# Four graph layers on one core: layer 1's first norm with centred weights, two-operation Sturm steps, and a wider window beside the last group of layer 0

## The chip, the cores and the metric

The kernel runs on one core of a Trainium2 chip. The metric is the device time of one execution in microseconds (us). The program is one launch; everything is fp32. The core has five engines that work side by side, each through its own queue in order: TensorE (PE, with the loads of its stationary operand shown apart as PEld), VectorE (DVE), ScalarE (ACT), GpSimd (POOL) and SyncE (SP), which here issues the DMAs.

## The reference, cut to what matters

128 graphs of 64 nodes with 256 features share one 64 x 64 weighted adjacency matrix. Four layers follow, each of the form x + f(relu(layernorm(x))).

```python
def _L0_gnn_ref(x, adj, ...):           # two graph convolutions, then LSTMs over windows of 1, 2, 3 and 4 nodes
    h = relu(einsum('ts,bsh->bth', adj, x @ Wg0 + bg0))
    h = relu(einsum('ts,bsh->bth', adj, h @ Wg1 + bg1))
    for p in range(1, MAX_SKIP + 1):
        ...                             # the last state of each window replaces that node's row of h
def _L1_gnn_ref(x, L, adjacency, Wc, bc, g1, be1, ...):
    lam_max = eigvalsh(L)[-1] + 1e-08
    L_norm = 2.0 * L / lam_max - eye(N)
    h = einsum('mn,bnf->bmf', L_norm, x) @ Wc + bc
    h = relu(_layernorm(h, g1, be1))
    x1 = h + x
    ...                                 # attention of 4 heads, layernorm, MLP with gelu, layernorm
def _L2_gnn_ref(h, adj_matrix, W, a):   # graph attention: softmax over neighbours
    ...
def _L3_gnn_ref(features, A, W1, b1, W2, b2):
    ...
    _, U = eigh(L_norm)                 # all 64 eigenvectors of the normalised Laplacian
    agg = einsum('mn,bnd->bmd', U.T, features)
    out = relu(agg @ W1 + b1) @ W2 + b2
    return einsum('nm,bmd->bnd', U, out)
```

## The kernel before, in words

**A planner writes the order.** The kernel first records all operations (`Plan.record`, from line 114) with their engine, group, tiles and dependencies. Then `Plan.schedule` (line 227) lays them out as a list scheduler, with a cost for each kind of operation (`Plan.cost`, line 176), and `issue` (line 338) emits them in that order. So each engine's queue is the planner's order, and every instruction carries line 344 in the profile: one tells groups apart by their tiles, not by lines. The planner picks for each engine the operation that can start first, and among those that can start at once the one of the lowest rank (line 328). An operation that depends on one of its own engine is planned to start at that one's end, some 0.11 us behind its cost.

**Groups.** Layer 0 works on 8 groups (0 to 7, NG = 8) of 8 tiles of 128 rows. The weights of layers 1 to 3 are prepared in one group of their own (WEIGHTS), layer 2's attention tiles are cleared in another (ATTN), and layers 1 to 3 run on 16 groups of 4 tiles (REST onward), each from its input to its output. The eigenvalue work (EIG) is a group aside, of the lowest rank on all engines but TensorE: it fills gaps of VectorE beside layer 0.

**The window.** `window(oldest)` (line 968) says how far ahead of the oldest unfinished group others may begin. While layer 0's last group (7), WEIGHTS or ATTN is the oldest, it gives `REST + 1 - oldest`: one group of layers 1 to 3 may work, and the loads of one more may be issued. After that it is 8 groups.

**Buffers.** The pool "big" has 12 tiles of 128 x 1024, and gets more as others are done with their memory: 10 in `arena` when the EIG group has ended, and those in whh[3], sums and mids (lines 963 to 966) when all of layer 0 has ended. While a layer-0 group is the oldest, 7 big tiles and 3 of the 8 PSUM banks are kept in reserve for it (`reserve`, line 971).

**Layer 0's memory for later weights.** Wc, Wq, Wk and Wv are loaded into the memory of Wih1, which the LSTM of windows of two (p = 1) has read for the last time; Wo and row vectors (bc, g1, be1, ...) into Wih2, further vectors and small tiles into Whh2, which windows of three (p = 2) read last. WEIGHTS needs the finished eigenvectors for `ursum` and `C3` (lines 1428 to 1434), so it ends after EIG.

**Sturm sweeps** (lines 634 to 663), in EIG: bisection finds the eigenvalues. Each of 9 sweeps evaluates, for 3 x 7 shifts on 64 partitions, a recurrence of 64 steps: a product DX x PL[k], from the second step on also a product PL[k-1] x E2 and a difference, each on 64 x 21 elements, and every eighth step a rescaling. Then the sign changes are counted.

**Layer 1's first norm** (lines 1523 to 1535). `relu_norm` makes h, `mix_fm` multiplies by the scaled Laplacian (`lapb`), `proj_tm` by Wc, two tiles of 256 columns into one PSUM bank, and VectorE adds bc on the way to x1. Then `norm(x1)`: `ln_stats` (line 1195) issues for each tile bn_stats and bn_aggr on VectorE, then four small operations on GpSimd (one of them the power -0.5), and ScalarE applies scale and bias to four tiles. VectorE multiplies by g1, GpSimd adds be1, VectorE takes the maximum with 0 and adds h.

Of the kernel before, what the change touches and what calls it, by code (L numbers as in the profile page):

```python
# [8 lines left out]
ALU = mybir.AluOpType  # L9
AF = mybir.ActivationFunctionType  # L10
AX = mybir.AxisListType

N = 64
KS = 7
# [332 lines left out]
def eig_decomp(plan, room, adj, adjT, ident, idf, ones):  # L347
# [17 lines left out]
    def scope():  # L365
        inner.reset([0])
        return inner
# [4 lines left out]
    def W(shape, name, bufs=None):  # L372

        if bufs is None:
            bufs = 2 if shape[-1] < N or name == "lab" else 1
        ring = kept.setdefault((name, tuple(shape)), [])
        if len(ring) < bufs:
            ring.append(room.tile(shape))
        else:
            ring.append(ring.pop(0))  # L380
        return ring[-1]
# [245 lines left out]
    V.tensor_copy(lo, l1.to_broadcast([N, 3]))  # L627
    C = 3 * KS
    ph = scope()
    PL = ph.tile([N, N + 1, C])  # L630
    V.memset(PL[:, 0, :], 1.0)
    DX = ph.tile([N, N, 3, KS])
    SG = ph.tile([N, N + 1, C])
    for s_ in range(NSWEEP):
        V.tensor_scalar(w, w, 1.0 / (KS + 1), None, op0=ALU.mult)
        x = W([N, 3, KS], 'x')
        V.tensor_scalar(x, c['ramp'], w, None, op0=ALU.mult)
        V.tensor_add(x, x, lo.unsqueeze(2).to_broadcast([N, 3, KS]))
        for l in range(3):
            V.tensor_mul(DX[:, :, l, :], BM[:, l, :].unsqueeze(2).to_broadcast([N, N, KS]), x[:, l, :].unsqueeze(1).to_broadcast([N, N, KS]))  # L640
            V.tensor_sub(DX[:, :, l, :], DM[:, l, :].unsqueeze(2).to_broadcast([N, N, KS]), DX[:, :, l, :])
        DXf = DX.rearrange('p k l s -> p k (l s)')
        for k in range(N):
            V.tensor_mul(PL[:, k + 1, :], DXf[:, k, :], PL[:, k, :])
            if k:
                b = W([N, 3, KS], 'b', 2)
                V.tensor_mul(b, PL[:, k - 1, :].rearrange('p (l s) -> p l s', l=3), E2[:, :, k - 1:k].to_broadcast([N, 3, KS]))
                V.tensor_sub(PL[:, k + 1, :], PL[:, k + 1, :], b.rearrange('p l s -> p (l s)'))
            if k % 8 == 7 and k < N - 1:
                mm = W([N, C], 'mm')  # L650
                V.tensor_reduce(mm, PL[:, k:k + 2, :].rearrange('p k c -> p c k'), op=ALU.max, axis=AX.X, apply_absolute_value=True)
                V.tensor_scalar(mm, mm, 1e-30, None, op0=ALU.max)
                V.reciprocal(mm, mm)
                V.tensor_mul(PL[:, k:k + 2, :], PL[:, k:k + 2, :], mm.unsqueeze(1).to_broadcast([N, 2, C]))
        V.tensor_scalar(SG, PL, 0.0, None, op0=ALU.is_lt)
        NE = DXf
        V.tensor_tensor(NE, SG[:, 1:, :], SG[:, :N, :], op=ALU.not_equal)
        ct = W([N, 3, KS], 'ct')
        V.tensor_reduce(ct.rearrange('p l s -> p (l s)'), NE.rearrange('p k c -> p c k'), op=ALU.add, axis=AX.X)
        V.tensor_tensor(ct, ct, li.unsqueeze(2).to_broadcast([N, 3, KS]), op=ALU.is_le)  # L660
        sm = W([N, 3], 'sm')
        V.reduce_sum(sm, ct, axis=AX.X)
        V.scalar_tensor_tensor(lo, sm, w, lo, op0=ALU.mult, op1=ALU.add)
# [269 lines left out]
def gnn_kernel(ctx: ExitStack, tc: tile.TileContext, a, out):  # L933
# [32 lines left out]
    more(mids, tuple(range(NG)))  # L966

    def window(oldest):
        return max(oldest, 0) + 2 - oldest if oldest < NG - 1 else REST + 1 - oldest if oldest < REST else 8

    def reserve(kind, oldest):
        if oldest < NG:
# [204 lines left out]
    def tm(n=HT, f=D):  # L1177

        return plan.value("big")[:, :n * f].rearrange("p (t f) -> p t f", f=f)
# [214 lines left out]
    ctile = lambda shape, src: load(room.tile(shape), src)  # L1394
    Wc, Wq, Wk, Wv, W1, W2, Wo = (wtile(a[n]) for n in ("Wc", "Wq", "Wk", "Wv", "W1", "W2", "Wo"))
    bc, g1, be1, bo, g2, be2, b2, g3, be3 = (btile(a[n]) for n in ("bc", "g1", "be1", "bo", "g2", "be2", "b2", "g3", "be3"))
    b1 = ctile([P, 4], a["b1"])

    g2c, be2c = (ctile([P, 2], a[n].rearrange("o (c p) -> p (o c)", p=P)) for n in ("g2", "be2"))
# [98 lines left out]
    def norm(t):  # L1498

        sc, bi = ln_stats(t)  # L1500
        for i in range(HT):
            ACT.activation(t[:, i, :], t[:, i, :], AF.Identity, scale=sc(i), bias=bi(i))
# [20 lines left out]
    def layer1(x):  # L1523
        h = relu_norm(x)
        lx = mix_fm(h, lambda t: lapb)
        x1 = tm()
        for t0 in (0, 2):
            ps = proj_tm(lambda c, t: lx[:, c, tok(t)], Wc, 2, t0)
            V.tensor_add(x1[:, t0:t0 + 2, :], ps.rearrange("p (t f) -> p t f", t=2), vec(bc, 2))
        norm(x1)  # L1530
        for t0 in (0, 2):
            xp, hp = x1[:, t0:t0 + 2, :], h[:, t0:t0 + 2, :]
            V.tensor_mul(xp, xp, vec(g1, 2))
            G.tensor_add(xp, xp, vec(be1, 2))
            V.scalar_tensor_tensor(xp, xp, 0.0, hp, op0=ALU.max, op1=ALU.add)
        x1T = to_fm(x1)
        qT, kT, v = fm(), fm(), tm()
        R = pieces(lambda c, n: x1T[:, c, n * HT * P // 2:(n + 1) * HT * P // 2], G)
        proj_fast(fastp["Wq"], R, qT)
        proj_fast(fastp["Wk"], R, kT)  # L1540
        for t0 in (0, 2):
            evac(pair(v, t0), proj_tm(lambda c, t: x1T[:, c, tok(t)], Wv, 2, t0), 1)
        for t0 in (0, 2):
            G.tensor_add(x1[:, t0:t0 + 2, :], x1[:, t0:t0 + 2, :], vec(bo, 2))


        ps = [bank("qk") for m in range(2)]
        with plan.burst():
            for b, m, r in [(b, m, r) for b in range(2 * HT) for m in range(2) for r in range(2)]:
                PE.matmul(ps[m][half(r ^ m), bat(b)], qT[half(r), m, bat(b)], kT[half(r), m, bat(b)], start=True, stop=True)  # L1550
        s = tm(4 * HT, N)
        for m in range(2):
            sm = s[:, m * 2 * HT:(m + 1) * 2 * HT, :]
            V.scalar_tensor_tensor(sm, ps[m].rearrange("p (b k) -> p b k", k=N), 0.125, vec(mask1, 2 * HT), op0=ALU.mult, op1=ALU.add)
            stat = plan.value("stat")
            softmax_shift(sm, stat[:, :2 * HT])
            ACT.activation(sm, sm, AF.Exp)
            ssum = stat[:, 2 * HT:4 * HT]
            V.reduce_sum(ssum, sm, axis=AX.X)
            V.reciprocal(ssum, ssum)  # L1560
            G.tensor_mul(sm, sm, ssum.unsqueeze(2).to_broadcast([P, 2 * HT, N]))

        pT = fm()
        for m in range(2):
            evac(pT[:, m, :], transposes([flat(s[:, (m * HT + t) * 2:(m * HT + t) * 2 + 2, :]) for t in range(HT)]), 1)
        oT = fm()

        po = [bank("o") for i in range(2)]
        with plan.burst():
            for m, t, i, r in [(m, t, i, r) for m in range(2) for t in range(HT) for i in range(2) for r in range(2)]:  # L1570
                PE.matmul(po[i][half(r), bat(m * HT + t)], v[half(i), t, bat(2 * m + r)], pT[half(i), m, bat(2 * t + (r ^ m))], start=True, stop=True)
        for i in range(2):
            evac(oT.rearrange("p c (t b n) -> p c t b n", t=HT, b=2)[:, :, :, i, :], po[i].rearrange("p (c t n) -> p c t n", c=2, t=HT), 1)
        x2 = tm()
        for t0 in (0, 2):
            ps = proj_tm(lambda c, t: oT[:, c, tok(t)], Wo, 2, t0)
            V.tensor_add(x2[:, t0:t0 + 2, :], ps.rearrange("p (t f) -> p t f", t=2), x1[:, t0:t0 + 2, :])
        norm(x2)
        x2T = fm()
        for c in range(2):  # L1580
            ACT.activation(x2T[:, c, :], transposes([x2[:, t, tok(c)] for t in range(HT)]), AF.Identity, scale=g2c[:, c:c + 1], bias=be2c[:, c:c + 1])
        V.tensor_mul(x2, x2, vec(g2))
        for t0 in (0, 2):
            G.tensor_add(x2[:, t0:t0 + 2, :], x2[:, t0:t0 + 2, :], vec(b2, 2))
        mT = [fm() for i in range(2)]
        for m in range(4):
            ACT.activation(mT[m // 2][:, m % 2, :], proj_fm(W1, x2T, m), AF.Gelu, bias=b1[:, m:m + 1])
        for t0 in (0, 2):
            ps = proj_tm(lambda c, t: mT[c // 2][:, c % 2, tok(t)], W2, 4, t0)
            V.tensor_add(pair(x2, t0), ps, pair(x2, t0))  # L1590
        for t0 in (0, 2):
            G.tensor_add(x[:, t0:t0 + 2, :], x[:, t0:t0 + 2, :], vec(be3, 2))
        norm(x2)
        for t0 in (0, 2):
            V.tensor_mul(x2[:, t0:t0 + 2, :], x2[:, t0:t0 + 2, :], vec(g3, 2))
            V.tensor_add(x[:, t0:t0 + 2, :], x[:, t0:t0 + 2, :], x2[:, t0:t0 + 2, :])
# [115 lines left out]
```

## Time and profile before

| | us |
|---|---|
| median of 3 runs | 2153.46 (2152.71 to 2155.54) |
| the profiled execution, its own time | 2151.09 |
| its span, from the first to the last instruction | 2149.3 |

| engine | busy us | instructions |
|---|---|---|
| PE (TensorE, matmuls) | 2102.0 | 16772 |
| PEld (loads of the stationary operand) | 1665.0 | 16772 |
| DVE (VectorE) | 1796.7 | 7434 |
| ACT (ScalarE) | 1124.1 | 2465 |
| POOL (GpSimd) | 708.4 | 1040 |

An fp32 matmul instruction leaves two records, so 16772 records are about twice the number of instructions. A row of a group of instructions gives the total busy time in which overlaps count once, the mean length of one in ns, and the idle time of the engine before them with what ended it. In the chain of waits, each piece is what the next one waited for. Layer 0's last matmuls end about 1361 us after the start of the span; layers 1 to 3 fill the rest.

### The profile page before, as it was taken

What the parts mean: (1) busy time and instruction counts of PE and PEld (TensorE: products, weight loads), DVE (VectorE), ACT (ScalarE), POOL (GpSimd) and SP (SyncE); (2) the same over time, 40 slices, a digit from 0 to 9 for tenths busy, and PEclk for the clock granted to TensorE, in tenths of its full rate; (3) what the DMA queues carried; (4) which work ended last, traced back from release to release, by engine and by line L of the source; (5) the groups of instructions that cost most, each with busy time, mean ns of one, the idle gap of its engine ahead of it and who ended that gap; (6) DMA issues with size and microseconds to landing.
All of it is one profiled execution on the core that took longest, in us unless ns stands there. A gap on an engine that the chain in (4) does not pass through costs nothing.

```text
span 2149.3 us, 46200 instructions
## 1 busy us (share of the span) xinstructions
PE 2102.0 (98%) x16772; PEld 1665.0 (77%) x16772; DVE 1796.7 (84%) x7434; ACT 1124.1 (52%) x2465; POOL 708.4 (33%) x1040
## 2 busy tenths in 40 slices
PE   9999999999999999999999999999999999999998
PEld 6688688688778778778778788877777877887776
DVE  5788888888999999989989898767787789876787
ACT  3354354355345345345345444566667666665783
POOL 7211211310110110110110002696556657864353
PEclk9999999999999999999999999999999999999999
DMA  5000100100100100100000111200000100000001
GB/s 206 1 3 22 42 2 22 41 1 21 40 1 21 40 1 21 40 1 21 26 1 21 50 40 51 90 1 2 21 22 21 41 22 21 11 12 11 2 2 60
DMA packets 44868, 57.70 MB, mean 27 GB/s; under 512 B 8928, under 2 KB 38496, under 8 KB 44640
## 3 DMA queue, kind: packets, MB, share of 16 engines
q1 hardware_dynamic: 43536, 53.71, 7.6%
q8 instruction: 131, 2.15, 0.4%
q10 hardware_dynamic: 1104, 1.05, 0.2%
q14 instruction: 97, 0.79, 0.1%
HBM read 37.53 MB, written 16.78 MB: 25 GB/s over the span
## 4 chain that ended last, share of the span: by engine, by line
PE 79%; DVE 11%; POOL 3%; issue 3%; ACT 2%; DMA 2%; SPq 0%; DVEq 0%; ACTq 0%; POOLq 0%
PE bank L344 79%; DVE stat L344 3%; DVE arena L344 3%; DVE big L344 3%; POOL stat L344 2%; DVE mids L344 1%; DVE sums L344 1%; DMA big<-in_x_dram 1%; ACT big L344 1%; ACT mids L344 1%; POOL arena L344 0%; ACT arena L344 0%; POOL big L344 0%; DVE Whh L344 0%; SPq L344 0%
## 5 line engine op out<-in xcount | busy, mean ns | idle before, releaser
L344 PE MATMUL bank<-big,Wih 128*128 128x256 f32 (+3 forms) x2408 | 731.7, 426 | 14.7 <-DVE arena L344 6.9
L344 PEld LDWEIGHTS bank<-big,Wih 128*128 128x128 f32 x2408 | 440.3, 190 | 183.0 <-issue 100.2
L344 ACT ACTIVATE mids<-bank,bl 128x256 f32<-128x256 f32 (+3 forms) x528 | 274.8, 527 | 385.7 <-PE bank L344 383.3
L344 PE MATMUL bank<-big,Whh 128*128 128x256 f32 (+2 forms) x1692 | 448.0, 366 | 1.5 <-DVE big L344 1.4
L344 DVE TENSOR_TENSOR arena<-arena 64x21 f32<-64x21 f32 (+5 forms) x2253 | 372.3, 195 | 29.5 <-POOL arena L344 1.2
L344 PEld LDWEIGHTS bank<-big,Whh 128*128 128x128 f32 x1692 | 306.8, 190 | 40.6 <-issue 8.6
L344 PE MATMUL bank<-big,sums 128*128 128x168 f32 (+2 forms) x1472 | 263.8, 321 | 1.6 <-ACT big L344 1.5
L344 POOL TENSOR_SCALAR stat<-stat 128x4 f32<-128x4 f32 (+1 forms) x228 | 69.8, 307 | 514.0 <-DVE stat L344 499.2
L344 PEld LDWEIGHTS bank<-big,sums 128*128 128x128 f32 (+1 forms) x1472 | 220.5, 185 | 17.4 <-issue 3.4
L344 ACT COPY mids<-bank 128x168 f32<-128x168 f32 (+2 forms) x427 | 146.2, 364 | 151.9 <-PE bank L344 146.0
L344 DVE TENSOR_TENSOR big<-mids 128x512 f32<-128x512 f32 (+2 forms) x256 | 141.5, 562 | 33.9 <-ACT mids L344 30.7
L344 ACT ACTIVATE mids<-mids,bl 128x336 f32<-128x336 f32 (+3 forms) x192 | 102.1, 539 | 78.7 <-DVE mids L344 74.9
L344 DVE TENSOR_TENSOR mids<-bank,mids 128x168 f32<-128x168 f32 (+2 forms) x322 | 116.1, 368 | 25.1 <-PE bank L344 17.6
L344 DVE SCALAR_TENSOR_TENSOR arena<-arena 64x1 f32<-64x1 f32 (+15 forms) x565 | 124.3, 243 | 6.1 <-POOL arena L344 2.5
L344 POOL TENSOR_TENSOR stat<-stat,mhalf 128x4 f32<-128x4 f32 (+1 forms) x114 | 123.9, 1088 | 5.6
L344 ACT ACTIVATE mids<-big 128x256 f32<-128x256 f32 (+2 forms) x176 | 89.4, 510 | 62.7 <-DVE big L344 46.3
L344 POOL TENSOR_TENSOR big<-big 128x168 f32<-128x168 f32 (+1 forms) x30 | 21.4, 726 | 272.5 <-DVE arena L344 105.7
L344 DVE TENSOR_SCALAR arena<-arena 64x1 f32<-64x1 f32 (+8 forms) x533 | 102.4, 199 | 8.3 <-POOL arena L344 0.4
L344 DVE TENSOR_TENSOR big<-big,mids 128x256 f32<-128x256 f32 (+2 forms) x194 | 95.2, 492 | 9.7 <-ACT mids L344 8.5
L344 PE MATMUL bank<-Wih,big 128*128 128x256 f32 x384 | 94.1, 383 | 3.1 <-DVE big L344 0.9
L344 POOL TENSOR_TENSOR arena<-arena 64x1 f32<-64x1 f32 (+1 forms) x70 | 46.8, 669 | 145.9 <-ACT arena L344 105.8
L344 ACT ACT_TABLE_LOAD x55 | 70.6, 1283 | 35.9 <-PE bank L344 18.0
(371 smaller groups left out, 3747.9 us busy)
## 6 DMA issues: line engine op xcount, KB each, us to landing
big<-in_x_dram SPq DMA_DIRECT2D x30, 512.0 KB, 5.5
put<-big SPq DMA_DIRECT2D x16, 512.0 KB, 2.8
arena<-put SPq DMA_DIRECT2D x8, 512.0 KB, 6.6
out_dram<-arena SPq DMA_DIRECT2D x16, 256.0 KB, 2.3
Wih<-in_WihT_dram SPq DMA_DIRECT2D x3, 1024.0 KB, 11.9
Whh<-in_WhhT_dram SPq DMA_DIRECT2D x3, 1024.0 KB, 13.9
big<-put SPq DMA_DIRECT2D x5, 512.0 KB, 5.4
out_dram<-big SPq DMA_DIRECT2D x10, 256.0 KB, 2.2
```

The source lines that it names most:

```text
L344: getattr(self.engines[op.eng], name)(*map(real, args), **{k: real(a) for k, a in kw.items()})
```

## The change

Three edits. In the Sturm sweeps the coefficients of both terms lie side by side in one tile CO (the second plane is DX, the first is -E2, written once), so that one product of 64 x 42 and one addition of 64 x 21 make a step; the first row of PL is set by GpSimd in each sweep instead of once by VectorE; the signs are written over PL. In layer 1, the columns of Wc and bc have their mean over the 256 outputs taken off when the weights are prepared, so that the product has mean 0 in each row; ScalarE squares it into the PSUM bank that it came from, with the sum of the squares as a by-product, GpSimd makes the reciprocal root in two operations, and VectorE multiplies by it and g1 in one operation for each tile. The window lets eight groups of layers 1 to 3 begin where it let one.

```diff
     ph = scope()
     PL = ph.tile([N, N + 1, C])
-    V.memset(PL[:, 0, :], 1.0)
-    DX = ph.tile([N, N, 3, KS])
-    SG = ph.tile([N, N + 1, C])
+    CO = ph.tile([N, N, 2, C])
+    l3 = lambda t: t.rearrange('p k (l s) -> p k l s', l=3)
+    DX = l3(CO[:, :, 1, :])
+    for l in range(3):
+        V.tensor_scalar(l3(CO[:, 1:, 0, :])[:, :, l, :], E2[:, l, :M].unsqueeze(2).to_broadcast([N, M, KS]), -1.0, None, op0=ALU.mult)
...
-        DXf = DX.rearrange('p k l s -> p k (l s)')
-        for k in range(N):
-            V.tensor_mul(PL[:, k + 1, :], DXf[:, k, :], PL[:, k, :])
-            if k:
-                b = W([N, 3, KS], 'b', 2)
-                V.tensor_mul(b, PL[:, k - 1, :].rearrange('p (l s) -> p l s', l=3), E2[:, :, k - 1:k].to_broadcast([N, 3, KS]))
-                V.tensor_sub(PL[:, k + 1, :], PL[:, k + 1, :], b.rearrange('p l s -> p (l s)'))
+        G.memset(PL[:, 0, :], 1.0)
+        V.tensor_mul(PL[:, 1, :], CO[:, 0, 1, :], PL[:, 0, :])
+        for k in range(1, N):
+            b = W([N, 2, C], 'b', 2)
+            V.tensor_mul(b, PL[:, k - 1:k + 1, :], CO[:, k])
+            V.tensor_add(PL[:, k + 1, :], b[:, 0, :], b[:, 1, :])
...
-        V.tensor_scalar(SG, PL, 0.0, None, op0=ALU.is_lt)
-        NE = DXf
-        V.tensor_tensor(NE, SG[:, 1:, :], SG[:, :N, :], op=ALU.not_equal)
+        V.tensor_scalar(PL, PL, 0.0, None, op0=ALU.is_lt)
+        NE = CO[:, :, 1, :]
+        V.tensor_tensor(NE, PL[:, 1:, :], PL[:, :N, :], op=ALU.not_equal)
...
     def window(oldest):
-        return max(oldest, 0) + 2 - oldest if oldest < NG - 1 else REST + 1 - oldest if oldest < REST else 8
+        return max(oldest, 0) + 2 - oldest if oldest < NG - 1 else REST + 8 - oldest if oldest < REST else 8
...
+    mean = room.tile([P, 3])
+    for i, w in enumerate((Wc[:, 0, :], Wc[:, 1, :], bc)):
+        V.reduce_sum(mean[:, i:i + 1], w, axis=AX.X)
+        V.tensor_scalar(mean[:, i:i + 1], mean[:, i:i + 1], 1.0 / D, None, op0=ALU.mult)
+        V.tensor_scalar(w, w, mean[:, i:i + 1], None, op0=ALU.subtract)
...
         x1 = tm()
+        stat = plan.value("stat")
+        sq, rs = stat[:, :HT], stat[:, HT:2 * HT]
         for t0 in (0, 2):
             ps = proj_tm(lambda c, t: lx[:, c, tok(t)], Wc, 2, t0)
             V.tensor_add(x1[:, t0:t0 + 2, :], ps.rearrange("p (t f) -> p t f", t=2), vec(bc, 2))
-        norm(x1)
+            for t in (t0, t0 + 1):
+                ACT.activation(ps[:, (t - t0) * D:(t - t0 + 1) * D], x1[:, t, :], AF.Square, accum_out=sq[:, t:t + 1])
+        G.tensor_scalar(rs, sq, 1.0 / D, 1e-5, op0=ALU.mult, op1=ALU.add)
+        G.tensor_tensor(rs, rs, mhalf, op=ALU.pow)
         for t0 in (0, 2):
             xp, hp = x1[:, t0:t0 + 2, :], h[:, t0:t0 + 2, :]
-            V.tensor_mul(xp, xp, vec(g1, 2))
+            for t in (t0, t0 + 1):
+                V.scalar_tensor_tensor(x1[:, t, :], x1[:, t, :], rs[:, t:t + 1], g1, op0=ALU.mult, op1=ALU.mult)
             G.tensor_add(xp, xp, vec(be1, 2))
             V.scalar_tensor_tensor(xp, xp, 0.0, hp, op0=ALU.max, op1=ALU.add)
```

## The prediction

> **What bounds the kernel now.** I read the page's busy times first, then the table of busy time by stretch, then the waits of TensorE in the stretches where it is idle, last the timeline at those places. Page, part 1:
>
> ```profile
> PE 2102.0 (98%) x16772; PEld 1665.0 (77%) x16772; DVE 1796.7 (84%) x7434; ACT 1124.1 (52%) x2465; POOL 708.4 (33%) x1040
> ```
>
> TensorE has an instruction under way for all but 47.3 us of the span of 2149.3. The busy time by stretch (columns: stretch, length, then busy us and instructions of PE, PEld, DVE, ACT, POOL, granted clock, DMA share, GB/s) says where those lie: layer 0 in its steady part, its last group, the start of layers 1 to 3, their steady part, their end.
>
> ```profile
> 550.00:1195.00 645.00, 638.70 (x3843) 502.30 (x3842) 592.56 (x2722) 287.54 (x652) 67.13 (x96) 1.00 0.06 19
> 1195.00:1361.00 166.00, 159.47 (x846) 132.67 (x845) 132.56 (x591) 71.24 (x161) 27.93 (x41) 1.00 0.15 46
> 1361.00:1500.00 139.00, 132.51 (x1381) 108.00 (x1380) 106.85 (x278) 87.30 (x178) 112.12 (x139) 1.00 0.10 36
> 1500.00:2100.00 600.00, 591.21 (x6611) 465.12 (x6610) 479.82 (x1395) 409.65 (x743) 353.38 (x482) 1.00 0.06 17
> 2100.00:2149.30 49.30, 39.39 (x671) 33.38 (x669) 34.23 (x103) 17.79 (x35) 17.65 (x25) 0.97 0.16 55
> ```
>
> PE idle is 6.3, 6.5, 6.5, 8.8 and 9.9 us. The change removes no matmul (8674 matmul instructions in both built programs), so these gaps, and what short waits hide in the overlap of matmuls, are all it can win. VectorE, 92% busy in the first stretch, is not the bound there: TensorE is idle for 1% of it. In the last group of layer 0, TensorE's waits are on VectorE:
>
> ```profile
> PE bank L344 <- DVE arena L344: 2.8, 4, 1.2
> PE bank L344 <- DVE big L344: 2.3, 3, 0.9
> PE bank L344 <- DVE mids L344: 1.1, 2, 1.0
> ```
>
> (us in total, times, longest.) The timeline of TensorE shows the only work of the later layers that fills it there: one mix with the Laplacian and eight products with Wc (16 records), of which these are the mix and the last six records:
>
> ```profile
> 1229.48 1.26 PE L344 MATMUL bank<-lapb,big 64*64 64x64 f32 x64
> ...
> 1266.48 1.46 PE L344 MATMUL bank<-Wih,big 128*128 128x256 f32 x6
> ```
>
> [...] a 128x256 record is 380 ns long, but four take 1.03 us, a start every 216 ns. So a wait of up to 380 - 216 = 164 ns leaves no idle time. [...] nine 64x21 operations in a row take 1.29 us, 143 ns each. [...]
>
> **The change, part by part.** Durations are of the rows of the profiled execution.
>
> *Sturm steps.* 9 sweeps of 63 steps: three 64x21 operations become one 64x42 and one 64x21. The row has 208 ns for one 64x42 against 178 for a 64x21, so in a row some 143 + 30 = 173. A step saves 3 x 143 - 143 - 173 = 113 ns, 567 steps 64 us of VectorE between 555 and 1290 us. Not brought forward: the planner places each step by its chain of two dependent operations, which is as long as before, and in both built programs the third, fifth and seventh sweep stand ahead of the same layer-0 groups. VectorE gets slack instead. TensorE is idle for 6.3 us of 550 to 1195, at group boundaries, where the chain of waits is mostly bn_stats (3.23 us for 16) and has some 0.3 to 0.6 us of Sturm work. Four boundaries: -1.5 us (0 to -4). The nine memsets that go to GpSimd (a 64x2 memset there takes 93 ns) are covered by the comparisons and reductions of a sweep (a 64x1344 reduction is 3.08 us).
>
> *Last group of layer 0, 1195 to 1361.* Three things. (a) The centring: three sums, three scalings and three subtractions on VectorE. By a 128x512 reduction (672 ns, so about half: 0.35), a 64x1 operation (0.17) and a 64x128 one (285 ns, taken for 256 columns as 0.3), 3 x 0.82 = 2.5 us. They stand in VectorE's queue inside the last step of p = 2: `mean` lies in Whh2, which that step still reads, and the third sum needs bc, whose load has 3.9 us from issue to landing. Behind them are the additions of that step, and TensorE waits for those. 0 to +6 us; I take +1.5, since matmuls issued ahead cover part. (b) No product with Wc can run before that, and the built order has neither mix nor Wc product ahead of layer 0's last LSTM matmul. The filler, 1.26 us + 16 x 0.216 = 4.7 us, moves behind; where it stood TensorE may stand still. 0 to +4.7; I take +4. (c) VectorE has a quarter fewer Sturm operations in its queue: of the 6.2 us of waits above, -3 (0 to -5). Net +2.5 us.
>
> *More groups may begin.* Before, the window admits one group of layers 1 to 3 until the weights are all prepared, and the other inputs are fetched behind the write of the last x, at 1364.56 us (5.67 us to landing in the chain), then normalised; TensorE is idle for 6.5 us of 1361 to 1500. In the new order five inputs stand ahead of the last layer-0 fetch in SP's queue, and three mixes follow at once on layer 0's last LSTM matmul, with 24 Wc products (10.4 us) around the last transposes. At the later rate (8.8 of 600 us) 139 us would have 2.0 us idle: -4.5 visible, somewhat more hidden; but the one admitted group filled TensorE until the next group's first mix, about 1374 us, so not all of it was a cold start. -4 us (-8 to +4).
>
> *Layer 1's norm*, 16 groups. VectorE: minus 4 x (404 + 155) for statistics, minus 2 x 740 for the g1 product, plus 4 x 489 for the fused product: -1.76 us a group, -28 us. ScalarE: minus 4 x 596, plus 4 x (413 + 188 for reading the accumulator; no row has a 256-wide Square into PSUM, so this is the nearest, and it may be shorter): about 0. The built program has 6 table loads fewer (49 against 55), 6 x 1.28 = -7.7 us of ScalarE. GpSimd: two of four small operations go, 0.31 + 0.26 a group, -9 us in all. All of it lies beside matmuls (VectorE is at 80% from 1500 to 2100, ScalarE 68%, GpSimd 59%). The chain of a group becomes shorter by 1 to 2 us, but up to eight groups share TensorE. The squares hold the product's bank 1.2 us longer, 32 times: 38 us of bank time of 8 banks x 790 us, under 1%. Of the 8.8 us of idle time I take -2.5 (-5 to +4).
>
> *Start and end.* TensorE's first 511 us and last 178 us of work stand in the same order in both: 0 (-2 to +2).
>
> Sum: -1.5 + 2.5 - 4 - 2.5 = -5.5 us. The profiled execution took 2151.1 us (2149.3 and 1.8 around it), so 2145.6; the median shown, 2153.46, stands 2.4 above that execution, so **2148.0 us**.
>
> **Rivals.**
>
> *Slower: VectorE stands on the load of bc.* VectorE takes its queue in order, so a late bc stops the LSTM behind it: the full 3.9 us of landing plus 2.5 us of centring reach TensorE, the 4.7 us of filler are lost, and VectorE's relief comes elsewhere. +11.1 in the last group; with -2 for the start and nothing else, 2153.5 + 9 = 2162. For it: before, the loads into Wih2 and Whh2 left SP between 1288 and 1308 us, just in that step, and TensorE was already waiting on VectorE there. Against it: VectorE arrives with less behind it. It decides once TensorE's idle time from 1195 us to the end of layer 0 exceeds 6.5 by more than the start gains, some 4 us. A start with three groups in step, on a GpSimd that had 45.1 busy of 50 us from 1400 to 1450, would push the same way by up to 4 us.
>
> *No difference: the gains cancel.* Lost filler and centring (+5.5) against the start (-4) and VectorE's relief (-1.5 to -3): about 2153. For it: every part but the start works on an engine that is not the bound.
>
> *The order pays more than counted:* every visible gap in the start and half of those in the steady part close with the shorter chain: -1.5 + 0 - 6.5 - 4.5 = -12.5, 2141.
>
> **How the numbers follow.** About 0.2% (4.3 us) can be told from no change here. Likeliest, with its own range 2142 to 2154: 0.40, two thirds of it below 2149.2. More than counted: 0.17. Cancel: 0.18, of it 0.02 slower by over 0.2%. Slower: 0.25. So faster 0.44, same 0.29, slower 0.27. The range reaches from a little below the third case to the second end, 2137 to 2162.
>
> **What would show it.** Right: PE busy stays at 2102 within a few us; VectorE falls by about 64 + 28 - 3 = 89 us; in layer 0 before the last group TensorE's idle time falls slightly; in the last group it does not fall, with waits of TensorE on VectorE around the products with Whh2; behind it idle time falls to some 2 us in 139; ScalarE is unchanged but for the table loads. Wrong: a VectorE wait of several us on the load of bc; idle time behind layer 0 as large as before; waits of TensorE on ScalarE for banks that squares hold; or a steady part that moves by more than 5 us either way, which would mean that the order there, and not the operations, decides.

## The result and the profile after

The changed kernel takes 2158.72 us (median of 8 runs, 2157.42 to 2161.47). Beside it the kernel before took 2153.54 (8 runs). The ratio is 1.0024, with a 95% interval of 1.0013 to 1.0035: slower by about 5 us, where the forecast was 2148.0 and most likely faster. The profiled execution took 2159.02, with a span of 2157.2 against 2149.3: 7.9 us more.

The first part of the page after (busy us, share of the span, instructions of each engine), and the view of the granted clock of the core:

```profile
PE 2108.3 (98%) x16772; PEld 1673.0 (78%) x16772; DVE 1767.2 (82%) x6782; ACT 1114.2 (52%) x2523; POOL 695.6 (32%) x1017
core 0: 2157.2 us, clock 0.993
```

TensorE has the same 16772 records and is busy 6.3 us longer. VectorE falls by 29.5 us, not by 89. The mean granted clock is 0.993; for before this view says 0.998. The busy time by stretch, cut where layer 0's last LSTM product ends in each kernel (1362.2 us here, 1358.7 before):

```profile
550.00:1195.00 645.00, 638.94 (x3838) 502.00 (x3837) 574.32 (x2170) 286.49 (x649) 66.75 (x104) 1.00 0.06 19
1195.00:1364.00 169.00, 159.34 (x865) 132.53 (x867) 139.54 (x644) 75.86 (x172) 37.01 (x55) 0.98 0.21 67
1364.00:1500.00 136.00, 131.13 (x1412) 108.83 (x1402) 97.64 (x204) 82.58 (x192) 94.43 (x109) 0.99 0.03 9
1500.00:2100.00 600.00, 590.71 (x6450) 465.61 (x6449) 462.79 (x1308) 394.92 (x767) 346.52 (x459) 1.00 0.05 17
2100.00:2157.20 57.20, 46.59 (x802) 39.84 (x800) 42.43 (x129) 24.02 (x48) 20.67 (x30) 0.97 0.17 57
```

Length minus PE busy gives TensorE's idle time: 6.1, 9.7, 4.9, 9.3 and 10.6 us, where before has 6.3, 6.5, 6.5, 8.8 and 9.9. With the first 550 us (8.4 against 9.3) the sum is 48.9 against 47.3. So idle time explains 1.6 of the 7.9 us; the other 6.3 are in busy time. The clock column points to a cause: 0.98 and 0.99 in the second and third stretch, where before has 1.00. The trace's clock records put TensorE at half clock for 30.8 us of the span here and for 10.2 us before. By an estimate from these records the 20.5 us more cost at most half of that, 10.3 us, so they have room for the 6.3.

The largest of the added stretches is in the last group of layer 0. TensorE (columns: start, us, operation; in brackets the idle time before, and what ended it):

```profile
1283.76 0.45 PE L344 MATMUL bank<-big,Whh 128*128 128x168 f32 x2
1287.63 0.93 PE L344 MATMUL bank<-big,Wih 128*128 128x168 f32 x2 [3.42 <-DVE mids L344]
1288.36 0.77 PE L344 MATMUL bank<-big,Whh 128*128 128x168 f32 x2
1288.92 0.77 PE L344 MATMUL bank<-big,Wih 128*128 128x168 f32 x2
```

A row of two records takes 0.45 us ahead of the wait and 0.77 behind it. The clock records have half clock from 1286.8, inside the wait, for 6.8 us. What VectorE did in that time:

```profile
1283.84 0.68 DVE L344 TENSOR_TENSOR arena<-arena 64x6 f32<-64x6 f32 x2
1284.44 2.54 DVE L344 RECIPROCAL arena<-arena 64x384 f32<-64x384 f32 x1
1286.90 0.45 DVE L344 TENSOR_TENSOR mids<-mids 128x336 f32<-128x336 f32 x1
```

One reciprocal of the eigenvalue work, untouched by the change, stands in the queue ahead of an LSTM addition that ScalarE and then TensorE wait for (ScalarE for 2.83 us, TensorE for 3.42). VectorE kept to its queue: in both profiled executions its records, those of accumulator reads aside, name the same tiles in the same order as the built program, 7090 of them before and 6438 here. The kernel before has the same instruction, with matmuls queued beside it; its timeline:

```profile
1276.96 2.56 DVE L344 RECIPROCAL arena<-arena 64x384 f32<-64x384 f32 x1
```

No TensorE wait of over 0.6 us follows it within 4 us there.

### The profile page after: what moved, and what is told of

Same layout as the page of the kernel before. It is cut to its first block, busy times and chain, and to the rows that moved or that the text cites. A ratio compares the mean times of both kernels' runs of the same rounds, so it can differ in the third digit from the quotient of the medians.

```text
span 2157.2 us, 45549 instructions
## 1 busy us (share of the span) xinstructions
PE 2108.3 (98%) x16772; PEld 1673.0 (78%) x16772; DVE 1767.2 (82%) x6782; ACT 1114.2 (52%) x2523; POOL 695.6 (32%) x1017
## 4 chain that ended last, share of the span: by engine, by line
PE 86%; DVE 9%; ACT 2%; DMA 2%; issue 1%; POOL 1%; SPq 0%; DVEq 0%; ACTq 0%
PE bank L344 86%; DVE big L344 3%; DVE arena L344 2%; DVE stat L344 2%; DMA big<-in_x_dram 1%; DVE mids L344 0%; ACT big L344 0%; POOL stat L344 0%; DVE sums L344 0%; DMA big<-put 0%; SPq L344 0%; ACT L344 0%; ACT mids L344 0%; DVE Whh L344 0%; DMA Wg<-in_Wg_dram 0%
## 5 line engine op out<-in xcount | busy, mean ns | idle before, releaser
L344 PE MATMUL bank<-big,Wih 128*128 128x256 f32 (+3 forms) x2352 | 718.2, 428 | 17.7 <-DVE big L344 4.4
L344 PEld LDWEIGHTS bank<-big,Wih 128*128 128x128 f32 x2352 | 432.4, 191 | 188.8 <-issue 101.5
L344 PE MATMUL bank<-big,Whh 128*128 128x256 f32 (+2 forms) x1852 | 416.5, 340 | 2.7 <-DVE big L344 2.6
L344 DVE TENSOR_TENSOR arena<-arena 64x42 f32<-64x42 f32 (+6 forms) x1684 | 352.2, 210 | 43.6 <-POOL arena L344 1.4
L344 PEld LDWEIGHTS bank<-big,Whh 128*128 128x128 f32 (+1 forms) x1852 | 294.4, 183 | 36.0 <-issue 4.3
L344 POOL MEMSET arena<- 64x2 f32 (+6 forms) x81 | 8.7, 112 | 465.7 <-DVE arena L344 465.5
L344 DVE SCALAR_TENSOR_TENSOR arena<-arena 64x1 f32<-64x1 f32 (+16 forms) x569 | 126.8, 246 | 6.2 <-POOL arena L344 2.5
L344 DVE TENSOR_TENSOR mids<-bank,mids 128x168 f32<-128x168 f32 (+1 forms) x315 | 111.6, 359 | 23.1 <-PE bank L344 10.2
L344 ACT ACTIVATE mids<-big 128x512 f32<-128x512 f32 (+2 forms) x176 | 89.6, 510 | 69.5 <-DVE big L344 58.4
L344 POOL TENSOR_TENSOR arena<-arena 64x1 f32<-64x1 f32 x66 | 44.2, 670 | 125.1 <-ACT arena L344 106.4
```

Of the source, the lines that this page charges most:

```text
L344: getattr(self.engines[op.eng], name)(*map(real, args), **{k: real(a) for k, a in kw.items()})
```

## The experiments

Eighteen kernels, each beside the kernel before on the same chip. Letters in the expectations: A, a few TensorE gaps of the new order and the half clock that they set off; B, longer Sturm steps; C, the centring and the load of bc; D, centring that leaves no products with Wc ahead of layer 0's end; E, the squares; F, a planner's order that any edit deals anew; G, costs that belong to the edited operations. A margin is a constant of the planner that can move the order and no operation.

| run | what | median us | ratio (95%) | mean clock |
|---|---|---|---|---|
| e1_sturm | Sturm steps alone | 2154.05 | 1.0002 (0.9994 to 1.0010) | 0.9954 |
| e2_norm | centring and norm alone | 2181.16 | 1.0128 (1.0115 to 1.0142) | 0.9915 |
| e3_window | window alone | 2161.22 | 1.0043 (1.0030 to 1.0055) | 0.9934 |
| e4_cut | changed, reciprocal cut | 2153.79 | 1.0003 (0.9995 to 1.0011) | 0.9961 |
| e5_centring | centring alone | 2188.41 | 1.0157 (1.0143 to 1.0171) | 0.9896 |
| e6_early | centring placed early, norm | 2172.56 | 1.0086 (1.0072 to 1.0100) | 0.9938 |
| e7_early_cut_one | e6 with Sturm and cut | 2173.09 | 1.0086 (1.0072 to 1.0099) | 0.9935 |
| e8_early_cut_two | e7, window of two | 2177.71 | 1.0108 (1.0094 to 1.0122) | 0.9920 |
| e9_null_before | before, margin 0.06 | 2170.29 | 1.0077 (1.0065 to 1.0090) | 0.9920 |
| e10_null_after | changed, margin 0.06 | 2154.34 | 1.0006 (0.9998 to 1.0015) | 0.9949 |
| e11_before_cut | before, reciprocal cut | 2153.61 | 1.0001 (0.9992 to 1.0009) | 0.9955 |
| e12_after_cut_10 | changed, cut, margin 0.10 | 2152.69 | 1.0000 (0.9992 to 1.0008) | 0.9965 |
| e13_before_10 | before, margin 0.10 | 2154.23 | 1.0001 (0.9993 to 1.0009) | 0.9959 |
| e14_after_10 | changed, margin 0.10 | 2160.30 | 1.0030 (1.0019 to 1.0041) | 0.9944 |
| e15_before_04 | before, margin 0.04 | 2161.62 | 1.0032 (1.0020 to 1.0044) | 0.9937 |
| e16_after_04 | changed, margin 0.04 | 2158.13 | 1.0023 (1.0015 to 1.0031) | 0.9959 |
| e17_cut_best | changed, cut, three margins | 2154.27 | 1.0001 (0.9993 to 1.0009) | 0.9964 |
| e18_cut_second | changed, cut, two margins | 2154.23 | 1.0002 (0.9994 to 1.0011) | 0.9948 |

### One part of the change at a time

e1, e2 and e3 are the kernel before with one part of the diff each: the Sturm hunks; the centring and the norm; the window line.

> The two-operation Sturm steps alone. Theory A (the loss lies in a few TensorE gaps of the new order, each made longer by a stretch at half clock that it sets off, and the wider window sets these gaps up): within 3 us of the kernel before. Theory B (in a row the new step is longer: 438 ns a step in the changed kernel's trace against 413 ns before, so VectorE's eigen chain ends later and its long operations fall among the additions of the LSTM): 3 to 6 us slower. Theory C (centring, the load of bc and the lost filler): no change. The prediction's own step: 1.5 us faster. All: VectorE's busy time falls by some 15 to 25 us and not by 64.

> Centring of Wc and bc and the new norm of the Chebyshev product alone, window and Sturm steps as before. Theory A and theory B: within 3 us of the kernel before. Theory C: 4 to 6 us slower, with TensorE idle behind VectorE's sums and subtractions in the last group of layer 0. The prediction's own steps: 3 us faster (+1.5 +4 for the last group if the filler is lost here too, -2.5 for the norm, so between -2.5 and +3).

> The wider window alone (REST + 8). Theory A: 3 to 6 us slower, since the inputs and first operations of several later groups stand among those of the last group of layer 0, and VectorE's long eigen operations then stand ahead of its additions: one TensorE wait of 2 us or more before 1360 us and a granted clock below 0.997. Theory B and C: no loss; the prediction's own step: 4 us faster.

**Sturm: no change.** Theory B falls. VectorE's busy time falls by 17.7 us (1779.0 in all), inside the 15 to 25 expected. The timelines at about 700 us, before and then after, show a row of steps that nothing interrupts:

```profile
700.16 2.98 DVE L344 TENSOR_TENSOR arena<-arena 64x42 f32<-64x42 f32 x21
```

```profile
701.02 2.17 DVE L344 TENSOR_TENSOR arena<-arena 64x42 f32<-64x42 f32 x10
```

21 operations are seven old steps, 10 are five new ones. From start to start, by the single records, a step takes 413 ns before and 438 after. In the old step the product with DX needs the last difference and starts 208 ns behind it, the next difference 207 ns behind that product; the product with E2 needs neither and stands in the first of these waits (98 ns behind the difference). So it takes no time of its own in such a row. In the new step the product of 64 x 42 and the addition follow each other by 230 and 208 ns: the same two waits, and 22 ns for the wider product. The operation that was saved was free here.

**Norm alone: 27 us slower.** Theory C, at 4 to 6 us, had the direction and a fifth of the size; A, B and the prediction's own step missed. Two lines of e2's TensorE timeline:

```profile
1364.84 1.03 PE L344 MATMUL bank<-Wih,big 128*128 128x256 f32 x4
1378.05 0.98 PE L344 MATMUL bank<-lapb,arena 64*64 64x64 f32 x16 [12.18 <-ACT arena L344]
```

Its one admitted group is through with its products, and the next group's input, fetched behind the write of the last x at 1366.98 us, is not yet normalised. The wait is 12.18 us long, and from 1370.3 on, inside it, TensorE is at half clock for 13.7 us. More is lost later; e2's busy time by stretch has 15.4 us idle here where before has 8.8:

```profile
1500.00:2100.00 600.00, 584.62 (x6206) 457.89 (x6205) 462.79 (x1255) 376.61 (x744) 357.88 (x455) 1.00 0.05 16
```

**Window alone: 7.4 us slower.** Theory A expected this, at 3 to 6 us, with the marks that it named. In e3's timelines of VectorE and then TensorE, the statistics of a second group's input stand among layer 0's additions, and TensorE waits:

```profile
1231.21 1.37 DVE L344 BATCH_NORM_STATS2 stat<-big 128x6 f32<-128x256 f32 x4
1232.78 0.66 DVE L344 TENSOR_TENSOR big<-mids 128x512 f32<-128x512 f32 x1
1233.35 1.40 DVE L344 BATCH_NORM_STATS2 stat<-big 128x6 f32<-128x256 f32 x4
```

```profile
1233.49 0.70 PE L344 MATMUL bank<-big,Whh 128*128 128x256 f32 x2 [0.78 <-DVE big L344]
1236.98 1.22 PE L344 MATMUL bank<-big,Whh 128*128 128x256 f32 x2 [2.36 <-DVE big L344]
```

The three parts alone add up to 0.2 + 27.3 + 7.4 = 35 us; together they cost 5. So the parts do not add up. Which of them offsets what the norm loses is not shown: no run has the norm with the wider window alone.

### The long reciprocal

```diff
-    V.reciprocal(RQ..., Q...)                        # 64 x 384
+    for i in range(0, N, 8):
+        V.reciprocal(RQ[:, i:i + 8]..., Q[:, i:i + 8]...)   # 64 x 48
```

> The changed kernel with the reciprocal of 64x384 cut into eight of 64x48, which may start beside the recurrence that makes their inputs. Theory A: the TensorE wait of 3.4 us at 1284 us and the 6.8 us at half clock behind it are gone (3.4 lost at half clock, and most of the wait): 3 to 6 us faster than the changed kernel, 2153 to 2156. Theory B: part of the loss stays, since the steps before it are as long: 2155 to 2158. Theory C: as the changed kernel, 2158 to 2160.

> The kernel before with the reciprocal of 64x384 cut into eight of 64x48. In its trace the long reciprocal stands at 1277 us, where TensorE had matmuls queued, so under theory A there is nothing to win: 2151 to 2156. If the cut by itself shortens the eigen chain for everyone: 2147 to 2150.

The pieces need only the part of the recurrence that makes their inputs, so the planner puts them in between (the last is 0.43 us long). The changed kernel with the cut takes 2153.79, 4.9 us less than without it and as much as the kernel before. e4 has 10.8 us of its span at half clock instead of 30.8, and around the old place its TensorE waits for VectorE are (us in total, times, longest):

```profile
PE bank L344 <- DVE mids L344: 1.7, 2, 1.2
PE bank L344 <- DVE big L344: 0.7, 1, 0.7
```

What the cut gains stands in busy time and not in idle time. TensorE is idle for 51.0 us of e4's profiled execution, 2.1 more than in the changed kernel's, and busy for 7.4 less:

```profile
PE 2100.9 (98%) x16772; PEld 1664.5 (77%) x16772; DVE 1770.0 (82%) x6789; ACT 1126.3 (52%) x2533; POOL 690.8 (32%) x1017
```

Of the 20 us less at half clock, 6.8 stood behind the reciprocal; most of the others stood further down.

In the kernel before, where the reciprocal does no harm, the cut changes nothing (e11). A second pair, further down, repeats it: with another planner margin the changed kernel takes 2160.30 whole (e14) and 2152.69 cut (e12), and in e14 TensorE waits of 1.38 and 1.72 us follow the reciprocal, then 3.4 us at half clock. The cut also lets the planner deal the rest of the order anew, so that the two pairs are not the removal of one wait alone; that both come down to the level of before, and that before does not move, is what speaks for the reciprocal. Against it as the only cause stands e16, a whole one further down: no TensorE wait over 0.6 us follows its reciprocal within 10 us, and it still takes 2158.13. So the long reciprocal is a likely and not a proven cause of the 5 us.

### Centring early or late

```diff
-    Wc, Wq, ... = ...; bc, g1, ... = ...; mean = room.tile([P, 3])
+    Wc = wtile(a["Wc"]); mean, bc = room.tile([P, 3]), btile(a["bc"])
+    Wq, ... = ...; g1, ... = ...
```

e5 has only the centring; e6 is e2 with this edit; e7 adds the Sturm steps and the cut; e8 is e7 with REST + 2.

> The centring of Wc and bc alone; norm, window and Sturm steps as before. Theory D (the centring waits for bc and for a place in Whh2, so no product with Wc can run ahead of layer 0's end, and with one admitted group nothing is left to fill TensorE until the next inputs are in): 2174 to 2182, with one TensorE wait of 10 to 13 us just behind layer 0's last product, as in the run with centring and norm. Theory E (the squares on ScalarE and the longer hold of the bank do it): within 3 us of the kernel before.

> Centring and norm without the wider window and the Sturm steps, but with mean and bc placed and loaded straight behind Wc, in the room that layer 0 leaves first, so that the centring can run about 60 us earlier and products with Wc stand ahead of layer 0's end again. Theory D: the wait of 12 us is gone, 2149 to 2156. Theory E: 2175 or more, as the run with centring and norm.

> Sturm steps, norm with mean and bc placed straight behind Wc, the reciprocal cut into eight, and the window of before (REST + 1). If the wider window's only worth was to repair what the late centring broke: 2147 to 2154, not slower than the kernel before. If the wider window is worth something by itself: 2156 or more.

> As the run before it with one group more (REST + 2): two groups' mixes with the Laplacian and their first products with Wc stand ahead of layer 0's end. If filler ahead of that end is what counts: 2145 to 2152, some 2 to 4 us faster than with REST + 1. If the early work of another group on VectorE (statistics, additions) stands in the way of the LSTM's additions, as theory A has it for the wider window: 2154 to 2160.

e5, 34 us slower, clears the squares of e2's loss: with the old norm it is larger. At the end of layer 0 TensorE waits 8.2 us (expected 10 to 13), and 24.6 us are idle from 1500 to 2100 us; the time lies above the 2174 to 2182 that theory D gave. So far the direction is theory D's. But e6 to e8, each 16 us or more above the times that the remedy gave them, refute it. In e6 the products with Wc stand ahead of layer 0's end again and the long wait is gone, and it is still 18.5 us slower than before; its stretch of later layers has 19.8 us idle:

```profile
1500.00:2100.00 600.00, 580.23 (x6255) 455.51 (x6254) 467.84 (x1270) 383.74 (x753) 342.92 (x447) 1.00 0.05 16
```

e7, without the wider window and with the reciprocal cut, is as slow. Its expectation would read that as a worth of the wider window by itself; but e7 differs from e4 in the place of the centring too, and no run has the early centring with the wide window, so this stays open. One group more of filler (e8) makes it worse, not better, with one wait of 6.8 us at 1423 us. In e6 and e7 the loss is spread over some ten waits of 1.3 to 2.5 us each, up to hundreds of microseconds behind the edit. A cost of the edited operations is hard to see in that, and it led to theory F.

### No operation changed

```diff
     def slack(op):
...
-        return 0.05
+        return 0.06
```

This is a constant by which the planner holds back what waits for another engine. e9 is the kernel before with this line alone, e10 the changed one. e12 and e13 to e16 move this or the margin ahead of TensorE's products in layer 0 (0.12).

> The kernel before with one constant of its planner moved: the margin that the planner adds to what other engines than TensorE wait for, 0.05 to 0.06. No instruction is added, removed or changed; only the order can change. Theory F (a list planner's order is re-dealt by any edit; how the groups of layers 1 to 3 fall against each other then sets TensorE's idle time, whatever the edit was for): 5 to 25 us off the kernel before, most of it behind 1361 us. Theory G (the times of the single parts measured so far are owed to the operations of those parts): within 2 us of the kernel before.

> The changed kernel with the same constant moved, 0.05 to 0.06. Theory F: several us off the changed kernel, in either direction; of the two directions the faster is taken, 2150 to 2157. Theory G: within 2 us of the changed kernel, 2157 to 2161.

> The changed kernel with the reciprocal cut into eight and the planner's margin before TensorE's matmuls of layer 0 at 0.10 instead of 0.12. Theory F: off the 2153.8 of the same kernel with 0.12 by several us in either direction, a chance of a version that is faster than both: 2147 to 2158. Theory G: 2152 to 2156.

> The kernel before with the planner's margin before TensorE's matmuls of layer 0 at 0.10 instead of 0.12, no operation changed; a pair with the next run. Theory F: off the kernel before by several us, more likely slower, since the constants of before are those that suit its order: 2153 to 2172. Theory G: 2152 to 2155.

> The changed kernel with the same constant, 0.10. Theory F: off the changed kernel by several us: 2150 to 2165, and no fixed distance to its pair. Theory G, and a true loss of 5 us by the changed operations: 5 us above its pair.

> The kernel before with the margin for the other engines at 0.04 instead of 0.05, no operation changed; a pair with the next run. Theory F: slower than the kernel before by several us, 2156 to 2172. Theory G: 2152 to 2155.

> The changed kernel with the same constant, 0.04. Theory F: 2150 to 2168, no fixed distance to its pair. If the changed operations are worth something once both orders are dealt anew, this run is below its pair, as with 0.06 (2154.3 against 2170.3). Theory G and a true loss: 5 us above its pair.

The order by itself can move the time: with every operation as before, e9 is 17 us slower and e15 8 us. That is theory F, and G, which had both within 2 us, falls. It need not move it: e13 lies 0.9 us and e12 1.1 us from the kernels that they vary, where G had them too.

F placed e9's loss in idle time behind 1361 us. That was wrong twice. The first part of its page:

```profile
PE 2114.1 (97%) x16772; PEld 1671.8 (77%) x16772; DVE 1796.7 (83%) x7434; ACT 1110.0 (51%) x2451; POOL 700.4 (32%) x1040
```

Its span is 20.0 us longer than in before. Idle time is 7.9 of that, 4.7 of them from 550 to 1195 us (11.0 against 6.3), and longer busy time is 12.1, with 38.1 us at half clock instead of 10.2.

The same constant takes 4.4 us off the changed kernel: in e10 the whole reciprocal starts at 1275.0, and no wait above 0.8 us follows it up to 1290 us. The pairs, before and changed under one constant:

| constant | before | changed | difference |
|---|---|---|---|
| as it stands | 2153.5 | 2158.7 | +5.2 |
| 0.05 to 0.06 | 2170.3 | 2154.3 | -16.0 |
| 0.12 to 0.10 | 2154.2 | 2160.3 | +6.1 |
| 0.05 to 0.04 | 2161.6 | 2158.1 | -3.5 |

The mean difference is -2 us, and the four scatter about it with a standard deviation of 10. What the changed operations are worth with the order out of it, 5 us, none, or a loss, these runs do not settle.

### Further orders of the changed kernel

> The changed kernel with the reciprocal cut into eight and three planner margins moved (0.05 to 0.045, 0.12 to 0.09, 0.4 to 0.42). If the changed operations are worth the 5 us of the forecast once the order suits them: 2144 to 2151. If the order's spread is all there is: 2150 to 2165.

> The changed kernel with the reciprocal cut into eight and two planner margins moved (0.05 to 0.06, 0.12 to 0.09). As in the run before it: 2144 to 2151 if the changed operations are worth the forecast's 5 us once the order suits them, 2150 to 2165 if the order's spread is all there is.

Both miss the 2144 to 2151 that the forecast's gain would have given. Four orders of the changed kernel with the cut (e4, e12, e17, e18) lie between 2152.7 and 2154.3: as fast as before, none faster. Its four orders with the reciprocal whole (as it stands, e10, e14, e16) lie between 2154.3 and 2160.3.

## Why the prediction was wrong

The forecast was a sum of idle times. It came to -5.5 us; the profiled execution moved by +7.9. The median lies inside the range of 2137 to 2162, but at the end that the rival "slower" had set, and not by that rival's mechanism. By the forecast's own steps, measured in the profiled executions:

- **Sturm steps, -1.5: -0.2.** The saving of VectorE, 64 us, failed: 17.7 were measured with the steps alone. The sum took 143 ns for each operation in a row. That is an average over two dependent operations and one that stood in a wait of theirs; taken off, the latter saves nothing in a row, and the two left cost some 210 to 230 each. That fewer operations make a shorter row was the author's estimate; this trace has fewer operations and a longer row, 438 against 413 ns a step.
- **Last group, +2.5: +3.1 in idle time, for other reasons.** The centring on VectorE was sized right (0.73 + 0.20 + 0.42 + 0.61 + 0.14 + 0.33 = 2.4 us, 2.5 forecast) but cost TensorE nothing: VectorE waited 0.62 us for bc, and TensorE has no wait over 0.6 us between 1288 and 1316 us. So the first rival, slower by the load of bc, failed in its mechanism, although the result is on its side and its balance came true (3.1 us more idle here against 1.6 gained at the start). The lost filler was laid to the centring; with the window alone (e3) there is no mix and no product with Wc ahead of layer 0's end either. And VectorE was not relieved: TensorE's waits for it, 6.2 us before, are 9.5 here, where (c) forecast -3. The load of bc, and then the waits from 1195 to 1361 us:

```profile
1304.61 0.42 DVE L344 TENSOR_REDUCE Whh<-Wih 128x1 f32<-128x256 f32 x1 [0.62 <-DMA Wih<-in_bc_dram]
```

```profile
PE bank L344 <- DVE big L344: 4.4, 5, 1.4
PE bank L344 <- DVE mids L344: 3.9, 2, 3.4
PE bank L344 <- DVE arena L344: 1.2, 2, 0.8
```

- **Window, -4: -1.6** in idle time, and in return the statistics among layer 0's additions. How it acts together with the centring (27.3 and 7.4 us slower alone, 5 all together) could not be seen, because the parts were sized one by one.
- **Norm, -2.5: +0.5** in idle time. ScalarE fell by 9.9 us, about as forecast (six table loads fewer, the square 387 ns where 413 was taken); the forecast from the table loads was 7.7. VectorE's part failed in one term: the fused product was taken at 489 ns and averages 775. Of the 64, 39 take 425 to 485 ns, and the 25 that begin while a large GpSimd operation is under way take 591 to 1510 ns (last section). The rows, the two largest groups of four (tile, shape, count, busy us, mean ns):

```profile
L344 DVE SCALAR_TENSOR_TENSOR arena<-arena,stat,Wih 128x256 f32<-128x256 f32 x28 | 20.2, 773 | 0.9 <-POOL stat L344 0.9
L344 DVE SCALAR_TENSOR_TENSOR sums<-sums,stat,Wih 128x256 f32<-128x256 f32 x16 | 10.1, 684 | 1.6 <-POOL stat L344 1.6
```

- **Start and end, 0: -0.2** in idle time (the first 550 us and the part from 2100 us on). Right for the order. But 3.4 us of the added half clock are at 232 us, and another 3.4 at 894 us, in the steady part of layer 0; both follow waits that before has as well (2.19 us in both, and 2.69 there against 3.16 here). These 6.8 us are chance (last section): e11, with the order of before, has both stretches too.
- **Busy time, 0: +6.3.** The mark "PE busy stays at 2102 within a few us" failed. All idle steps together came to +1.6 where -5.5 was forecast, and this is the rest of the 7.9. The clock is the cause that the trace shows for it (20.5 us more at half clock, by the estimate above worth at most 10.3).

**The step that failed** is this last term, which the sum put at nothing: as no matmul is added or removed, it counted TensorE's idle time alone and left out the clock, and the busy time moved most. With it failed relief (c) of the last group, -3. In its place the runs show a wait of 3.42 us behind one reciprocal, with the longest of the added stretches at half clock, 6.8 us, beginning inside it; with the reciprocal cut, the median falls by 4.9 us and the busy time by 7.4. That the wait and its half clock alone make up the 5 us is not shown (e16).

Below both lies an assumption that the forecast writes out for the Sturm steps alone ("in both built programs the third, fifth and seventh sweep stand ahead of the same layer-0 groups") and otherwise makes silently: that the eigenvalue operations keep their places among the LSTM's additions. The built order, which it read for sweeps, inputs and mixes, also has the places of single operations over 2 us; the forecast does not name the reciprocal. The last of the forecast's marks of being wrong, "that the order there, and not the operations, decides", is near to what the null edits e9 and e15 showed, but the steady part of layers 1 to 3 that it speaks of moved by 0.5 us only.

## What to carry to other kernels

Where a list planner writes the order, an edit is two changes: its operations, and a new deal of everything else. Measure the second by itself, with an edit of a planner constant that changes no operation; here it was worth up to 17 us, three times the change under study. Before adding parts up, look in the built order for single instructions longer than the slack of those behind them: with the 2.54 us reciprocal cut into eight, both pairs came back to the level of before. And count a wait of TensorE twice where the clock records show half clock behind it, once as idle time and once for the clock: here a wait of 3.42 us and 6.8 us at half clock, in which a row of two records took 0.77 us instead of 0.45.

## What the hardware showed

**Half clock behind idle time of TensorE.** This is counted in the clock records and TensorE's records of the 20 profiled executions. In each of them the half-clock stretches start whole multiples of 3.4133 us apart (91 stretches, to within 4 ns), and those that end inside the span are 3.4, 6.8, 10.2 or 13.7 us long. Cut into pieces of 3.4133 us on the grid of these starts, all 66 pieces at full clock with 1.98 us or more of idle time were followed by half clock, and none of the 12266 with less than 1.25 us; of those between, 26 were and 108 were not. In before, two pieces were followed by half clock, with 1.91 and 1.93 us idle, and the most idle of the others has 1.70; in the changed kernel eight were, with 1.71 to 3.41 us, and the most idle of the others has 1.42. The idle time was not always in one wait: in the changed kernel, waits of 0.99 and 1.68 us within 3.4 us (1365.4 to 1368.8), with matmuls in between, were followed by 3.4 us at half clock.

So in these two executions it made a difference where a wait fell on the grid, which lies 2.75 us behind the span's start in before and 3.39 us in after. One and the same wait, at 232 us in before and then in after:

```profile
232.06 1.12 PE L344 MATMUL bank<-big,Wih 128*128 128x512 f32 x2 [2.19 <-DVE big L344]
```

```profile
231.99 2.02 PE L344 MATMUL bank<-big,Wih 128*128 128x512 f32 x2 [2.19 <-DVE big L344]
```

The same two records take 1.12 us there and 2.02 here. In before a piece ends at 231.4 us with 1.57 us of idle time, and the rest of the wait falls into the next; in after the whole wait lies in a piece that ends at 232.1, where 3.4 us at half clock begin. The scatter of one kernel goes with the clock too: of 121 runs of the kernel before in these experiments, the 10 at a mean clock of 0.994 have a median of 2156.0 us and the 5 at 0.998 one of 2151.7, 1.1 us for each 0.001 (the correlation of time and clock is -0.64). The change's 8 runs average 0.9938 against 0.9961 for those 121: by an estimate from that slope 2.5 of the 5 us, and with TensorE as the bound throughout at most 5.0.

**VectorE beside GpSimd.** In the trace of the changed kernel the 64 fused products are of one shape. Of the 17 that overlap no GpSimd operation, all take 426 to 485 ns; of the 47 that overlap one, 22 take 425 to 480 ns as well, two about 590, and 23 take 943 to 1510 ns. All 25 longer ones begin while a GpSimd TENSOR_TENSOR of 128x256 or 128x512 is under way, and end 279 to 286 ns after it; none of the other 39 begins so. Of these 39, 15 overlap a GpSimd operation of 128x512 that begins later and others one of 128x4, and all take 425 to 485 ns. What makes the 25 longer is not shown beyond this coincidence in time. One case, VectorE and then GpSimd:

```profile
1843.67 0.97 DVE L344 SCALAR_TENSOR_TENSOR sums<-sums,stat,Wih 128x256 f32<-128x256 f32 x1
```

```profile
1843.64 0.73 POOL L344 TENSOR_TENSOR mids<-mids 128x256 f32<-128x256 f32 x1
```
